# Factored self-attention as guest work of a cross attention: shifted keys and values moved by DMA, with separate tiles and chains

## The chip, the cores and the metric

The kernel runs on one core of a Trainium2 chip, as one launch. The metric is the device time of that launch in microseconds (us), the median of several executions. TensorE (PE) multiplies matrices, VectorE (DVE), ScalarE (ACT) and GpSimd (POOL) work on tiles in on-chip memory (SBUF) and on matmul results (PSUM), and SyncE (SP) issues most DMA transfers. The engines run in parallel. Each executes its own instructions in order and waits on semaphores for the others.

## The reference

A pre-norm decoder of twelve layers works on x, 8 batches x 256 rows x 128 channels in fp32, with a context of 8 x 512 x 128. Each layer is `x = x + layer(layernorm(x))`; attention has 16 heads of 8 channels. Three layers matter here.

```
x = x + L1_ffn(_layernorm(x))        # r = sigmoid(xr @ Wr.T); out = r * (relu(xk @ Wk.T)**2 @ Wv.T)
                                     # xr, xk: mixes of a row with the row before it
x = x + L2_attn(_layernorm(x))       # q, k, v = x @ W_qkv + b_qkv, 16 heads
                                     # softmax(where(fenwick_mask, q k^T * scale, -inf)) v, then W_proj
x = x + L2_xattn(_layernorm(x), ctx) # softmax(q k^T * scale) v over 512 context rows, no mask
```

In the mask of `L2_attn` row i sees itself and the rows i - 1, i - 2, i - 4, ..., i - 128. So a query has at most nine keys, at offsets 0, 1, 2, 4, 8, 16, 32, 64 and 128, and the layer can be computed from nine shifted copies of keys and values with no matrix of scores. That is what "factored" means in this document. Keys at negative rows are masked by a large negative number.

## The kernel before, in words

x lies in SBUF as 16 tiles of 128 rows (two to a batch), and its layernorm, transposed, as `E.xt(b)`, 128 channels x 256 rows. `E.xt(b, o)` is the same shifted by o rows.

**The head loop.** The second cross attention, `_l2_xattn` (L773), runs `_heads_attention` (L469): a loop over 128 head steps t, 16 for each of 8 batches. At step t it computes the scores of head t twice. First with queries on partitions, two matmuls `mh_sps` of 128x512, from which DVE takes the row maxima (`mh_nm`, L533). Every fourth step POOL splits four heads' maxima (`mh_hi`, L540), TensorE transposes them (`mh_mps`), and a DMA on ACT's queue writes them as two more rows of the queries. Eight steps behind, the scores come again with keys on partitions (`mh_bsps`), less the maxima, and ACT takes their exponential (`mh_e`, L587). Every fourth step `mh_ops` sums values over keys. In the steps h = 6 to 13 of batch b the keys, queries and values of batch b + 1 are projected and spread over partitions by twelve DMAs of SP (L425, L430). All matmuls and transposes go through `hd.mm` and `hd.turn_over` (L451, L454), which keep TensorE in the order in which the program is written; on the other engines a scheduler orders the instructions by their dependences.

**The guest.** The loop carries other layers' work between its own instructions: a generator, `guest`, is advanced `pace(t)` times a step (`visit`, L706), here 1.25. This guest is `rest()` in `_middle` (L1242): `_l1_ffn` for batch pairs 1 to 3, `_l2_attn` for batches 2 to 7, then the rounding of weights of a later layer (`_l2_ffn_weights`). Batches 0 and 1 of `_l2_attn` were done before the loop. Batch b + 1 must be finished by the guest before step h = 9 of batch b; if it is not, the loop visits until it is (L695).

**The factored attention before**, `_l2_attn` (L1082), handles one tile of 128 rows at a time. It projects queries (`fa_q`), then, for each pair of offsets, keys and values of the shifted rows by matmuls of 128x256 into PSUM (`fa_kvps`, L1113): 8 for the upper and 9 for the lower tile of a batch. DVE multiplies keys by queries out of PSUM (`fa_pr`, L1114), ACT copies the values (`fa_v`, L1117). DVE sums over the channels of a head (L1123) and does the softmax over offsets (L1124 to L1134), POOL weights the values (L1136) and adds offsets 4 to 7 on 0 to 3 (L1138), and DVE adds the rest (L1144 to L1148). A transpose, the output matrix `wo`, the residual (L1156) and the next layernorm follow.

Of the kernel before, what the change touches and what calls it, by code (L numbers as in the profile page):

```python
# [30 lines left out]
F32 = mybir.dt.float32  # L31
# [23 lines left out]
OFFS = (0, 1, 2, 4, 8, 16, 32, 64, 128)  # L55
# [166 lines left out]
def _run(steps):  # L222
    for _ in steps:
        pass
# [120 lines left out]
class _Heads:  # L345
# [30 lines left out]
    def third(self, ctx):  # L376

        pool = ctx.enter_context(self.E.tc.tile_pool(name="hd3", bufs=1, side="right"))
        q = pool.tile([P, H, S], F32R, name="mh_q2")
        for i in range(0, H, 4):  # L380
            self.E.nc.scalar.copy(
                q[:, i : i + 4, :].rearrange("p h n -> p (h n)"), self.E.plain[:, 0:1].to_broadcast([P, 4 * S])
            )
        self.q.insert(0, q)

    def begin(self, layer, keys, bias=True):

# [395 lines left out]
def _l3_masks(E, ctx):  # L783

    nc = E.nc
    pool = ctx.enter_context(E.tc.tile_pool(name="km", bufs=1))
    mk = ctx.enter_context(E.tc.tile_pool(name="kmb", bufs=2))
    kb = pool.tile([P, B, 2, P], BF16, name="km")
    kt = pool.tile([P, B, 2], F32, name="km_t")
    with E.tc.tile_pool(name="km_raw", bufs=1) as rp:  # L790
        raw = rp.tile([P, B * S], I32, name="km_raw")
        nc.sync.dma_start(raw, E.ins["key_mask"].to_broadcast([P, B * S]))
        flat = kb.rearrange("p b i k -> p (b i k)")
        for i in range(0, B * S, 512):
            nc.vector.tensor_scalar(flat[:, i : i + 512], raw[:, i : i + 512], 0.0, NEG, ALU.is_equal, ALU.mult)
        rt = rp.tile([P, B * 2], I32, name="km_rt")
        nc.sync.dma_start(rt, E.ins["key_mask_t"])
        nc.vector.tensor_scalar(kt.rearrange("p b i -> p (b i)"), rt, 0.0, NEG, ALU.is_equal, ALU.mult)

    cq = pool.tile([P, 3, P], F32, name="km_cq")  # L800
    ck = pool.tile([P, 3, P], F32, name="km_ck")
    for c, pattern, cm in ((cq, -1, 1), (ck, 1, -1)):
        nc.gpsimd.memset(c, 0.0)
        for i in (0, 2):
            nc.gpsimd.affine_select(
                out=c[:, i, :], in_=c[:, i, :], compare_op=ALU.is_ge, fill=NEG, base=0,
                pattern=[[pattern, P]], channel_multiplier=cm,
            )
# [227 lines left out]
def _l1_ffn(E, ctx, side="left"):  # L1036
    nc, W = E.nc, E.w("L1_ffn")
    wk = ctx.enter_context(E.tc.tile_pool(name="rk", bufs=1, side=side))
    rest = wk.tile([P, 2], F32, name="rk_rest")
    for i, n in enumerate(("mu_r", "mu_k")):  # L1040
        nc.vector.tensor_scalar(rest[:, i : i + 1], W(n), -1.0, 1.0, ALU.mult, ALU.add)

    def unit(g):
        mixed = []
        for i, n in enumerate(("mu_r", "mu_k")):
            t = wk.tile([P, 2, S], F32, name="rk_t")
            nc.vector.tensor_scalar(t, E.xt2(g, 1), rest[:, i : i + 1], None, ALU.mult)
            m = wk.tile([P, 2, S], F32, name=f"rk_m{i}")
# [127 lines left out]
    return through  # L1176


def plain_pe(E):

    E.mm, E.transpose = E.nc.tensor.matmul, E.nc.tensor.transpose
    E.turn_over = lambda out, in_: E.nc.tensor.transpose(out, in_, E.ident)


def _middle(E, names, then):

    nc = E.nc
    plain_pe(E)  # L1190
    banks = lambda to, name, bufs, side="left": to.enter_context(
        E.tc.tile_pool(name=name, bufs=bufs, space=PSUM, side=side)
    )
    if names != MIDDLE:
        for n in names:
            with ExitStack() as scope:
                pg = E.mid_ln = banks(scope, "mid_pg", 6)
                E.banks = SimpleNamespace(fa=pg, rk=pg, ln=pg)
                unit = {
                    "L0_ffn": _l0_ffn, "L1_attn": _l1_attn, "L1_xattn": _l1_xattn, "L1_ffn": _l1_ffn,  # L1200
                    "L2_attn": _l2_attn,
                }[n](E, scope, *([pg] if n in MIDDLE[:3] else []))
                if n == "L2_attn":
                    _run(unit(0, 4))
                    continue
# [553 lines left out]
```

## Time and profile before

| | |
|---|---|
| median of 3 runs | 1801.41 us (1801.25 to 1802.14) |
| profiled execution | 1797.04 us |
| its span | 1795.3 us, mean granted TensorE clock 0.913 |
| second cross attention, first to last maxima | 910.8 to 1280.6 us |
| start of each batch's first step | 910.8, 960.7, 1008.6, 1061.2, 1108.6, 1162.5, 1218.6, 1253.5 us |
| SP queue | 44,720 packets, 56.99 MB, 12.0% of 16 DMA engines' span |

The profile is that of one execution, and its span is the time from the first to the last instruction; the execution's own time is 1.7 us longer. A "busy" time is the sum of an engine's instruction durations. A group such as `fa_kvps<-w_L_attn,xt 128x256 x204` names the written tile, what is read, the shape and the count; after the bar stand busy us and mean ns of one, and behind the next bar the idle time of the engine just before these instructions and what ended it. One fp32 matmul shows as two records, so x204 are 102 matmuls. A wait "A <- B: 28.5, 12, 3.8" is that A stood 28.5 us in all, 12 times, at most 3.8 us, and that B ended it. In the stage's stretches the columns are: stretch, its length, busy us (instructions) of PE, PEld (weight loads), DVE, ACT and POOL, granted clock of TensorE, share of the DMA engines, GB/s.

### The profile page before, as it was taken

The page shows a single profiled execution, that of the slowest core. Times are in us where ns is not written, and L with a number is a line of the kernel's source. Part 1 is how long each engine was busy: PE and PEld are TensorE (multiplying, and loading weights), DVE is VectorE, ACT ScalarE, POOL GpSimd, SP SyncE. Part 2 cuts the span into 40 slices and gives each one's busy share as a digit, 9 for nine tenths or more (in the row PEclk, how much of TensorE's full clock was granted, in tenths as well). Part 3 has the DMA queues.
Part 4 walks back from the last instruction along what each step waited for, and adds up shares of the span by engine and source line. Part 5 has one row for each costly group of instructions (what it writes and reads, how often), then busy time and mean ns, then how long its engine had stood idle before and what let it go on. Part 6 is the DMA issues. An engine that isn't in the chain of part 4 may idle for free. (4 is left out here: it accounts for less than half of the span.)

```text
span 1795.3 us, 29269 instructions
## 1 busy us (share of the span) xinstructions
PE 1476.0 (82%) x10103; PEld 1067.2 (59%) x10141; DVE 1149.9 (64%) x3861; ACT 871.3 (49%) x1806; POOL 502.6 (28%) x998
## 2 busy tenths in 40 slices
PE   5689999999989989787468888878846889898986
PEld 3456677766655556455346666656515677677753
DVE  4567666765636676777467776767566656466656
ACT  7245445555642345222635655456644556455531
POOL 3122222121111121323323333332113443344321
PEclk9899999999999999886779999989957999899997
DMA  4011101114100000000111001111002321122100
GB/s 152 13 36 35 25 15 37 35 28 150 23 1 1 1 1 1 0 1 1 24 46 32 24 22 37 37 37 45 10 3 66 101 53 37 52 58 54 29 1 24
DMA packets 47235, 60.42 MB, mean 34 GB/s; under 512 B 5232, under 2 KB 36976, under 8 KB 46448
## 3 DMA queue, kind: packets, MB, share of 16 engines
q1 hardware_dynamic: 44720, 56.99, 12.0%
q8 instruction: 80, 1.31, 0.3%
q10 hardware_dynamic: 2368, 1.57, 0.3%
q14 instruction: 67, 0.55, 0.1%
HBM read 14.50 MB, written 1.05 MB: 9 GB/s over the span
## 5 line engine op out<-in xcount | busy, mean ns | idle before, releaser
L451 PE MATMUL mh_sps<-mh_k,mh_q 96*128 96x512 f32 (+2 forms) x1024 | 323.7, 398 | 54.2 <-DMA mh_q<-mh_qp 24.1
L451 PE MATMUL mh_bsps<-mh_q,mh_k 128*128 128x256 f32 (+1 forms) x1536 | 355.1, 337 | 7.1 <-ACT mh_e L587 4.1
L587 ACT ACTIVATE mh_e<-mh_bsps 128x512 f32<-128x512 f32 x512 | 281.0, 599 | 118.0 <-PE mh_bsps L451 110.7
L451 PEld LDWEIGHTS mh_bsps<-mh_q,mh_k 128*128 128x128 f32 x1536 | 267.9, 199 | 32.2 <-issue 6.9
L451 PEld LDWEIGHTS mh_sps<-mh_k,mh_q 96*128 96x128 f32 x1024 | 173.1, 203 | 102.1 <-issue 44.6
L514 DVE CUSTOM_DVE_ANT_0 mh_rest<-mh_sps,mask_b 128x512 bf16<-128x512 f32 x256 | 167.2, 684 | 84.2 <-PE mh_sps L451 81.0
L451 PE MATMUL mh_ops<-mh_e,mh_v 128*32 128x256 f32 (+1 forms) x3072 | 193.7, 373 | 1.3 <-DVE mh_nm L514 0.8
L533 DVE TENSOR_REDUCE mh_nm<-mh_sps 128x1 f32<-128x512 f32 x256 | 165.1, 681 | 33.7 <-PE mh_sps L451 33.2
L574 ACT ACTIVATE mh_e<-mh_bsps 128x384 f32<-128x384 f32 x256 | 118.7, 493 | 59.5 <-PE mh_bsps L451 36.2
L197 POOL TENSOR_SCALAR ln_rstd<-ln_mv 128x2 f32<-128x2 f32 x96 | 22.0, 229 | 401.2 <-DVE ln_mv L195 400.9
L451 PEld LDWEIGHTS mh_ops<-mh_e,mh_v 128*32 128x32 f32 x3072 | 94.2, 111 | 66.1 <-ACT mh_e L574 5.5
L540 POOL CAST mh_hi<-mh_nm 128x8 fp32r<-128x8 f32 x128 | 24.8, 194 | 340.8 <-DVE mh_nm L514 208.9
L514 DVE CUSTOM_DVE_ANT_0 mh_rest<-mh_sps,causal 128x128 bf16<-128x128 f32 (+1 forms) x256 | 79.4, 352 | 53.9 <-PE mh_sps L451 51.3
L514 DVE CUSTOM_DVE_ANT_0 mh_rest<-mh_sps,km_q 128x128 bf16<-128x128 f32 (+1 forms) x256 | 79.5, 350 | 46.4 <-PE mh_sps L451 44.6
L215 ACT COPY xt<-ln_ps 128x256 f32<-128x256 f32 x96 | 36.0, 375 | 127.3 <-PE ln_ps L454 67.8
L552 ACT CAST mh_m<-mh_mps 8x256 fp32r<-8x256 f32 x128 | 46.1, 360 | 101.7 <-PE mh_mps L454 100.3
L620 ACT COPY mh_osb<-mh_ops 128x256 f32<-128x256 f32 x128 | 47.6, 372 | 83.3 <-PE mh_ops L451 83.1
L885 ACT ACTIVATE moe_si<-moe_gps 128x512 f32<-128x512 f32 x64 | 38.0, 597 | 102.0 <-PE moe_gps L883 81.3
L451 PE MATMUL mh_bsps<-mask_t,ident 128*128 128x512 bf16 x219 | 85.0, 388 | 0.4 <-ACT mh_e L587 0.4
L883 PE MATMUL moe_ups<-xt,w_L_ffn 128*128 128x512 f32 x128 | 68.9, 621 | 7.0 <-ACT moe_si L885 4.8
L454 PE MATMUL mh_mps<-ident,mh_nx 128*8 128x128 f32 x256 | 50.9, 281 | 28.8 <-POOL mh_nx L543 24.2
L201 DVE TENSOR_SCALAR ln_z<-x,ln_mv,ln_rstd 128x128 f32<-128x128 f32 x128 | 41.9, 368 | 50.5 <-POOL ln_rstd L198 50.5
(360 smaller groups left out, 3109.6 us busy)
## 6 DMA issues: line engine op xcount, KB each, us to landing
mh_k<-mh_kp SPq DMA_DIRECT2D x64, 256.0 KB
mh_q<-mh_qp SPq DMA_DIRECT2D x256, 64.0 KB
mh_k<-mh_kp SPq DMA_DIRECT2D x64, 128.0 KB
w_L_ffn<-in_w_L_ffn SPq DMA_DIRECT2D x2, 1558.0 KB
w_L_attn<-in_w_L_attn SPq DMA_DIRECT2D x2, 1056.0 KB
ctx_t<-in_ctx_t SPq DMA_DIRECT2D x4, 512.0 KB
mh_q<-mh_m ACTq DMA_DIRECT2D x128, 8.0 KB
w_L_ffn<-in_w_L_ffn SPq DMA_DIRECT2D x2, 687.0 KB
```

What stands on the lines that cost most here:

```text
L201: (engine or nc.vector).tensor_scalar(z[:, q, :], E.x[:, 2 * b + q, :], mv[:, q, 0:1], rstd[:, q : q + 1], ALU.subtract, ALU.mult)
L215: E.nc.scalar.copy(E.xt(b), ps.rearrange("p q t -> p (q t)"))
L451: return self.E.tc.keep_in_program_order(self.E.nc.tensor.matmul(*a, **kw))
L454: return self.E.tc.keep_in_program_order(self.E.nc.tensor.transpose(*a))
L514: nc.vector.tensor_tensor_reduce(rest[:, : scores.shape[1]], scores, lowered, -1.0, -FLOOR, ALU.add, ALU.min, accum_out=at)
L533: nc.vector.tensor_reduce(u.nm[:, c, col], ps, AX.X, ALU.max, negate=True)
L552: nc.scalar.copy(m, ps[:8].rearrange("p c q -> p (c q)"))
L574: nc.scalar.activation(e, ps, AF.Exp, scale=scale)
L587: nc.scalar.activation(e, ps, AF.Exp, scale=scale)
L620: nc.scalar.copy(osbs[b][:, u4 % 2, :], ops)
L883: nc.tensor.matmul(ps, W("w13")[:, o : o + P], xt, start=True, stop=True)
L885: nc.scalar.activation(si, pgate, AF.Silu)
```

## The change

1. In the guest, batches 2 to 7 of the factored attention are done by a new function, `_l2_attn_moved`, a batch (both tiles) at a time. It projects keys and values of each row once, and makes the eight shifted copies by SBUF-to-SBUF DMAs of SP, 15 for the keys and 15 for the values of a batch. Keys `fm_k` and values `fm_v` have one tile each, 128 x (2 x 9 x 128) fp32, whose rows before the start of a batch are zeroed once. The bias is added before the copies.
2. Keys and values are two chains of steps; each visit advances both by one. The chain of keys (`weigh`) carries `_l1_ffn` ahead of it and ends with the softmax weights of a batch. The chain of values (`apply`) waits for those in program order, weights both halves on POOL, and finishes the batch.
3. The pace of the guest in `_l2_xattn` goes from 1.25 to 1.6.
4. `_l1_ffn` puts `rk_k` and `rk_r` into the buffers of its mixed inputs. The pool of the first `_l2_attn` is closed before the guest's own pools are opened.
5. The causal additive blocks of layers `L3_attn` and `L3_xattn` are no longer built by `_l3_masks` within `L3_attn` (two memsets and four selects of POOL): the transposed one, `E.causal_t`, is built with the first heads' setup in `L2_ffn` (a memset and two selects), and `E.causal[0]` stands in for the other.

```diff
 def _l2_xattn(E, ctx):
-    _heads_attention(E, ctx, guest=guest, known=(0, 1), pace=lambda t: 1.25)
+    _heads_attention(E, ctx, guest=guest, known=(0, 1), pace=lambda t: 1.6)
...
-    cq = pool.tile([P, 3, P], F32, name="km_cq")
-    ck = pool.tile([P, 3, P], F32, name="km_ck")
-    for c, pattern, cm in ((cq, -1, 1), (ck, 1, -1)):
...
+    cq, ck = E.causal[0], E.causal_t
...
-        k = wk.tile([P, 512], F32, name="rk_k")
+        k = wk.tile([P, 512], F32, tag="rk_m1", name="rk_k")
...
-        r = wk.tile([P, 4, D], F32, name="rk_r")
+        r = wk.tile([P, 4, D], F32, tag="rk_m0", name="rk_r")
...
+    for a in (k, v):
+        nc.scalar.copy(a[:, 0, 1:, :].rearrange("p o c -> p (o c)"), E.plain[:, 0:1].to_broadcast([P, (NO - 1) * D]))
...
+    def move(a):
+        moves = []
+        for i, o in enumerate(OFFS):
+            if 0 < o < P:
+                moves.append((a[o:, :, i, :], a[: P - o, :, 0, :]))
+                moves.append((a[:o, 1, i, :], a[P - o :, 0, 0, :]))
+            elif o:
+                moves.append((a[:, 1, i, :], a[:, 0, 0, :]))
+        for i in range(0, len(moves), 3):
+            for to, of in moves[i : i + 3]:
+                nc.sync.dma_start(to, of)
+            yield
+        for _ in range(4):
+            yield
+
+    def weigh(b):
+        E.pre_add(b, W("bo"))
+        q = wk.tile([P, 2, D], F32, name="fm_q")
+        for s in range(2):
+            ps = E.banks.fa.tile([P, 2 * D], F32, tag="g", name="fm_qkps")
+            E.mm(ps, E.xt(b)[:, s * P : s * P + P], W("wqkv")[:, : 2 * D], start=True, stop=True)
+            nc.vector.tensor_tensor(k[:, s, 0, :], ps[:, D:], W("b")[:, D : 2 * D], ALU.add)
+            nc.vector.tensor_tensor(q[:, s, :], ps[:, :D], W("b")[:, :D], ALU.add)
+        at.projected = b
+        yield
+        yield from move(k)
+        while b > at.used + 2:
+            yield
+        sc = wk.tile([P, 2, NO, H], F32, name="fm_sc")
+        for s in range(2):
+            nc.vector.tensor_tensor(k[:, s, :, :], k[:, s, :, :], q[:, s : s + 1, :].to_broadcast([P, NO, D]), ALU.mult)
+            yield
+            nc.vector.tensor_reduce(sc[:, s, :, :], heads(k[:, s, :, :]), AX.X, ALU.add)
+            yield
...
+    def apply(b):
+        while b > at.projected:
+            yield
...
+        nc.vector.tensor_tensor(v[:, :, 0, :], ps, row, ALU.add)
+        yield
+        yield from move(v)
+        while b not in weights:
+            yield
+        sc = weights.pop(b)
+        for s in range(2):
+            nc.gpsimd.tensor_tensor(
+                heads(v[:, s, :, :]), heads(v[:, s, :, :]), sc[:, s, :, :].unsqueeze(3).to_broadcast([P, NO, H, DH]),
+                ALU.mult,
+            )
+
+            nc.gpsimd.tensor_tensor(v[:, s, :4, :], v[:, s, :4, :], v[:, s, 4:8, :], ALU.add)
+        at.used = b
+        for _ in range(5):
+            yield
+        o = wk.tile([P, 2, D], F32, tag="fm_q", name="fm_o")
+        nc.vector.tensor_tensor(v[:, :, :2, :], v[:, :, :2, :], v[:, :, 2:4, :], ALU.add)
+        nc.vector.tensor_tensor(o, v[:, :, 0, :], v[:, :, 1, :], ALU.add)
+        nc.vector.tensor_tensor(o, o, v[:, :, 8, :], ALU.add)
+        yield
...
+        chain = keys()
+        for done in values():
+            yield done
+            next(chain, None)
...
+        if guest:
+            last.close()
...
-            yield from fa(1, 3, _l1_ffn(E, own))
+            rk = _l1_ffn(E, own)
+            if guest:
+                yield from _l2_attn_moved(E, own)(2, B, rk)
+            else:
+                yield from fa(1, 3, rk)
```

More of the change, by code (lines that the diff above doesn't have):

```diff
@@ L384, in third @@
         self.q.insert(0, q)
+        t = self.E.causal_t = pool.tile([P, 3, P], F32, name="causal_t")
+        self.E.nc.gpsimd.memset(t, 0.0)
+        for i in (0, 2):
+            self.E.nc.gpsimd.affine_select(
+                out=t[:, i, :], in_=t[:, i, :], compare_op=ALU.is_ge, fill=NEG, base=0,
+                pattern=[[1, P]], channel_multiplier=-1,
+            )
     def begin(self, layer, keys, bias=True):
@@ L798, in _l3_masks @@
         nc.vector.tensor_scalar(kt.rearrange("p b i -> p (b i)"), rt, 0.0, NEG, ALU.is_equal, ALU.mult)
-    cq = pool.tile([P, 3, P], F32, name="km_cq")
-    ck = pool.tile([P, 3, P], F32, name="km_ck")
-    for c, pattern, cm in ((cq, -1, 1), (ck, 1, -1)):
[L803 to L808, printed above, removed]
+    cq, ck = E.causal[0], E.causal_t
     def key_bias(b):
@@ L1047, in unit @@
             nc.vector.tensor_scalar(t, E.xt2(g, 1), rest[:, i : i + 1], None, ALU.mult)
-            m = wk.tile([P, 2, S], F32, name=f"rk_m{i}")
+            m = wk.tile([P, 2, S], F32, tag=f"rk_m{i}", name=f"rk_m{i}")
             nc.vector.scalar_tensor_tensor(m, E.xt2(g), W(n), t, ALU.mult, ALU.add)
@@ L1176, in _l2_attn, with _l2_attn_moved, through, keys @@
     return through
+def _l2_attn_moved(E, ctx):
+    nc, W = E.nc, E.w("L2_attn")
+    one = ctx.enter_context(E.tc.tile_pool(name="fm1", bufs=1))
+    wk = ctx.enter_context(E.tc.tile_pool(name="fm", bufs=2))
+    scale = DH ** -0.5
+    NO = len(OFFS)
+    shape = [P, 2, NO, D]
+    k, v = one.tile(shape, F32, name="fm_k"), one.tile(shape, F32, name="fm_v")
+    for a in (k, v):
+        nc.scalar.copy(a[:, 0, 1:, :].rearrange("p o c -> p (o c)"), E.plain[:, 0:1].to_broadcast([P, (NO - 1) * D]))
+    heads = lambda a: a.rearrange("p o (h d) -> p o h d", d=DH)
+    weights, at = {}, SimpleNamespace(projected=-1, used=-1)
+    def move(a):
[31 more added lines that the diff above has]
+            yield
+        nc.vector.tensor_tensor(
+            sc[:, 0, :, :], sc[:, 0, :, :], W("fenwick").unsqueeze(2).to_broadcast([P, NO, H]), ALU.add
+        )
+        red = wk.tile([P, 2, H], F32, name="fm_red")
+        wide = red.unsqueeze(2).to_broadcast([P, 2, NO, H])
+        by_head = sc.rearrange("p s o h -> p s h o")
+        nc.vector.tensor_reduce(red, by_head, AX.X, ALU.max)
+        nc.vector.tensor_tensor(sc, sc, wide, ALU.subtract)
+        nc.scalar.activation(sc, sc, AF.Exp, scale=scale)
+        yield
+        nc.vector.tensor_reduce(red, by_head, AX.X, ALU.add)
+        nc.vector.reciprocal(red, red)
+        nc.vector.tensor_tensor(sc, sc, wide, ALU.mult)
+        weights[b] = sc
+        yield
+    def apply(b):
+        while b > at.projected:
+            yield
+        ps = E.banks.fa.tile([P, 2, D], F32, tag="g", name="fm_vps")
+        for s in range(2):
+            E.mm(ps[:, s, :], E.xt(b)[:, s * P : s * P + P], W("wqkv")[:, 2 * D :], start=True, stop=True)
+        row = W("b")[:, 2 * D :].unsqueeze(1).to_broadcast([P, 2, D])
+        nc.vector.tensor_tensor(v[:, :, 0, :], ps, row, ALU.add)
[4 more added lines that the diff above has]
+        sc = weights.pop(b)
+        for s in range(2):
+            nc.gpsimd.tensor_tensor(
+                heads(v[:, s, :, :]), heads(v[:, s, :, :]), sc[:, s, :, :].unsqueeze(3).to_broadcast([P, NO, H, DH]),
+                ALU.mult,
+            )
+            nc.gpsimd.tensor_tensor(v[:, s, :4, :], v[:, s, :4, :], v[:, s, 4:8, :], ALU.add)
+        at.used = b
+        for _ in range(5):
+            yield
+        o = wk.tile([P, 2, D], F32, tag="fm_q", name="fm_o")
+        nc.vector.tensor_tensor(v[:, :, :2, :], v[:, :, :2, :], v[:, :, 2:4, :], ALU.add)
+        nc.vector.tensor_tensor(o, v[:, :, 0, :], v[:, :, 1, :], ALU.add)
+        nc.vector.tensor_tensor(o, o, v[:, :, 8, :], ALU.add)
+        yield
+        ps = E.banks.fa.tile([P, 2, P], F32, tag="g", name="fm_tps")
+        for s in range(2):
+            E.turn_over(ps[:, s, :], o[:, s, :])
+        ot = one.tile([P, 2, P], F32, name="fm_ot")
+        nc.scalar.copy(ot, ps)
+        yield
+        ps = E.banks.fa.tile([P, 2, D], F32, tag="g", name="fm_yps")
+        for s in range(2):
+            E.mm(ps[:, s, :], ot[:, s, :], W("wo"), start=True, stop=True)
+        E.add(b, ps)
+        z = _norm(E, b)
+        yield
+        yield
+        yield
+        _normed(E, b, z, E.banks.ln, E.turn_over)
+        yield b
+    def through(first, end, ahead):
+        at.projected = at.used = first - 1
+        def keys():
+            for b in range(first, end):
+                if b % 2 == 0:
+                    yield from ahead(b // 2)
+                yield from weigh(b)
+        def values():
+            for b in range(first, end):
+                yield from apply(b)
+        chain = keys()
+        for done in values():
+            yield done
+            next(chain, None)
+    return through
```

## The prediction

> **What bounds the kernel now.** I read the page's busy shares first, then the stage that the change touches (the second cross attention, whose 128 head steps run from 910.8 to 1280.6 us by the starts of their maxima, DVE L533), cut into its batches, then that stage's groups by shape, and last its waits.
>
> ```profile
> span 1795.3 us, 29269 instructions
> ...
> PE 1476.0 (82%) x10103; PEld 1067.2 (59%) x10141; DVE 1149.9 (64%) x3861; ACT 871.3 (49%) x1806; POOL 502.6 (28%) x998
> ```
>
> TensorE leads over the kernel, but not fully. The chain that ended last reaches only into the final feed-forward layer and says nothing of this stage. So I go to the stretches: us, then busy time of PE, PEld, DVE, ACT, POOL (instructions), granted clock, DMA share, GB/s.
>
> ```profile
> 910.00:961.00 51.00, 38.58 (x221) 27.13 (x221) 38.06 (x92) 20.71 (x43) 16.83 (x29) 0.89 0.13 32
> ...
> 1219.00:1254.00 35.00, 31.59 (x239) 22.62 (x239) 25.97 (x62) 23.51 (x51) 8.12 (x22) 0.95 0.24 57
> 1254.00:1281.00 27.00, 26.68 (x241) 18.95 (x240) 20.27 (x42) 18.92 (x40) 2.83 (x12) 1.00 0.01 2
> 910.00:1219.00 309.00, 255.49 (x1794) 186.20 (x1794) 229.56 (x593) 165.79 (x362) 109.98 (x188) 0.93 0.14 32
> ```
>
> Sixteen head steps alone take 27 us with TensorE 99% busy (1254 to 1281). The six batches that carry the guest work take 309 us, 51.5 each, with PE at 83%, DVE at 74%. TensorE is the bound there, with DVE close behind; 53 us are PE's idle time. Where they come from:
>
> ```profile
> DVE fa_v L1144 <- POOL fa_v L1138: 28.5, 12, 3.8
> PEld mh_sps L451 <- DVE mh_nm L533: 28.2, 39, 5.1
> ...
> PE mh_sps L451 <- DVE mh_nm L533: 14.5, 9, 4.6
> ...
> PE mh_sps L451 <- DMA mh_q<-mh_qp: 7.6, 1, 7.6
> ```
>
> (total us, times, longest.) DVE stands in its queue on POOL's weighted values (12 tiles, 28.5 us); behind it stand the maxima of the heads, and TensorE waits for those. The guest's attention is on all three engines:
>
> ```profile
> L451 PE MATMUL fa_kvps<-w_L_attn,xt 128*128 128x256 f32 x204 | 55.6, 398 | 6.7 <-DVE x L1156 4.7 <-ACT fa_v L1117 1.6 <-DVE fa_q L1102 0.3
> ...
> L1114 DVE TENSOR_TENSOR fa_pr<-fa_kvps,fa_q 128x256 f32<-128x256 f32 x48 | 19.8, 416 | 3.0 <-PE fa_kvps L451 2.8
> L1117 ACT COPY fa_v<-fa_kvps 128x256 f32<-128x256 f32 x48 | 17.4, 369 | 25.2 <-DVE fa_pr L1114 25.2
> L1138 POOL TENSOR_TENSOR fa_v<-fa_v 128x512 f32<-128x512 f32 x12 | 15.3, 1274 | 0.6
> ...
> L1136 POOL TENSOR_TENSOR fa_v<-fa_v,fa_sc 128x1152 f32<-128x1152 f32 x6 | 13.1, 2190 | 20.6 <-DVE fa_sc L1134 12.3 <-DVE ln_mv L195 8.4
> ...
> L1123 DVE TENSOR_REDUCE fa_sc<-fa_pr 128x144 f32<-128x1152 f32 x6 | 8.1, 1348 | 0.1
> ```
>
> **The change, part by part.** Six batches (2 to 7) are converted.
>
> TensorE. The 102 shifted key-value products go (204 records; a pair of records fills about 0.515 us in the timeline, so 102 x 0.515 = 52.5 us), and 12 query products of 128x128 with them (4.6 us, x24 records). New are 12 of 128x256 (12 x 0.515 = 6.2) and 12 of 128x128 (12 x 0.28 = 3.4). Net -47.5 us of PE work in the bounding stretch: 255.5 becomes 208.
>
> DVE. Gone are two halves' products, reduces and softmax on one tile each: 19.8 + 1.7 products, 15.4 reduces (L1123), about 50 us of small softmax, bias and fold instructions; 86.8 us in all from the rows. New per batch: four bias adds (4 x 0.28), two products and two reduces of 128x1152 (4 x 1.35, by the L1123 row; the product has no row at this width), the softmax once on 128x288 (2.5), folds, bias and residual (2.4): 11.4, so 68.5 for six. Net -18 us: 229.6 becomes 211. The product's ends: 1.2 to 2.4 us (twice, if reading two SBUF operands beside POOL halves its rate), so 0 to +12 us over 12; I take 1.35.
>
> ACT loses 19 us of value copies (L1117) and gains two fills of about 1.04 us each; it is off the path. POOL: 45.4 us of multiply and fold become 12 x (2.19 + 1.27) = 41.5, but in blocks of two halves, 6.9 us, instead of 3.5. The heads' minima (L540, 0.2 us each) queue behind that block. They feed exponentials that run eight steps later, some 18 us, which covers it; uncovered, 6.9 less the 3.3 that it costs now, 3.6 us a batch.
>
> SP. 180 SBUF-to-SBUF copies are new, 30 a batch. One issue on SP takes 0.61 us in this trace, so 15 take 9.2 us per tensor. They share SP's queue with twelve key and query spreads per batch (0.61 to 1.28 us each), on which the heads of the next batch depend. SP has little else here. Spreads and copies overlap at batches 5 to 7 (steps 41 to 45, 74 to 77 of the new order); a spread then lands up to 9 us later, against three to seven steps (6 to 16 us) of slack. I count nothing for it; uncovered it is the 7.6-us wait on mh_q of the fence, perhaps three times: 0 to 23 us.
>
> How long a moved tensor takes. By the rows: 918 KB in 512-byte packets, about 1,800, at the 27 ns that this trace's 512-byte packets take, over 16 engines is 3 us, so SP's issuing decides: 10 us. A rule speaks against it: the Trainium skill, "DMA: Bandwidth & Descriptors", section "Why a DMA increments its semaphore by 16 and not by 1", says that a transfer from SP or ACT uses the largest number of engines up to 16 that divides the slowest dimension; 127 partitions go on a single engine, and a smaller number uses the lowest-numbered ones. The offset-1 copy is 127 rows x 2 = 254 packets on engine 0: 6.9 us; with its shares of the others (62 for the 124-row copy, 84 for the rest) engine 0 carries 400 packets, 10.8 us. The trace agrees with the rule in one place: the first queue of ACT, 2,368 packets, adds up only if the two-row copies of the minima go over two engines. Copies reuse eight semaphores in turn, so the ninth waits for the first: about 15 us from the first issue to the last landing. The chain leaves eight visits at 1.6 per step, five steps of 2.4 us: 12. So the product waits nothing by the row, 3 us by the rule. As DVE executes in order, the maxima behind it wait, then mh_sps on PE. I take the rule, with 2 us of PE time for each of six key copies: 12 us (range 0 to 36 with values' sums late as well, which wait only behind POOL).
>
> A new DVE block. In the built program's DVE order, batch 2's whole chain (products, reduces, softmax, 10.5 us) and its sum, which waits for POOL's 6.9 us, stand together after step 15's maxima and ahead of step 16's. Before, the same place waited 3.7 us. PE has three score banks of lead, so of the some 17 us I count 8 us. At batches 5 and 6 nine such instructions (8.5 us) stand together: 4 us each in the sum below for what exceeds a bank's lead, 8 in all.
>
> Pace 1.25 to 1.6 lets the guest end at step 93 instead of 104 and cancels three forced visits in steps 41 and 73. Work is compressed, not removed: nothing. The causal blocks: a memset and two selects move to the feed-forward layer and two memsets (0.42) and four selects (0.29 to 0.47) leave POOL in the third attention; POOL is 28% busy, no one waits: zero, at most 2 us either way. Shared mixing tiles make the ACT relu wait for its product's reader, same engine order as now: zero, at most 1 us a pair, 3.
>
> Sum on the profiled execution: -47.5 + 12 + 8 + 8 = -19.5 us. DVE's 18 us do not add to PE's. But the waits of the old arrangement (28.5 us in 12 on POOL, half of which reached PE) become six instead of twelve: -7. So -26 to -27; 1797.04 - 27 = 1770. The median of the runs, 1801.41, is 4.4 above the profiled execution; the same step from it gives 1774.
>
> **Rivals.**
> A. All cover holds: PE work is the bound, at its 83%: 208 / 0.83 = 251 instead of 309, so -58; some of it is lost to DVE at 84%: -45 to -58, 1743 to 1756. For it: PE is at 99% when alone. Against: DVE then has as much work as PE in each batch (35 us of each).
> B. DVE becomes the bound. 211 us of DVE work in blocks of 8 to 17 us; at the 74% it reaches now that is 285 us, -24; at 70%, 301, -8; 1777 to 1796. For it: the block at step 16. Against: most of DVE's idle time today is waiting for PE and POOL.
> C. Slower: engine 0 becomes the bound. 800 packets of two tensors per batch and about 8 us of spreads lie on it. At 27 ns that is 30 us; 46 ns, this trace's 1-KB packets, gives 45, still under 51.5; from 54 ns on it exceeds the batch of before, and the products, and all maxima behind them, run at its pace. This trace's 2-KB packets between tiles take 162 ns at the median, which speaks for such prices; at 60 ns it is 56 us a batch, 6 x 4.8 = +29: 1830. Against: 512 bytes are a quarter of those, and packets of that size show 27.
> D. The change does not reach the bound: if the new waits cancel the PE work, within 4 us of 1801. It follows from my sum with late copies at 36 us and both blocks fully on PE (+34): -47.5 - 7 + 36 + 34 = +15, so no change lies within reach.
>
> **How the numbers follow.** My sum 0.40, A 0.14, B 0.16, D 0.08 (no change), C with its neighbours 0.22. Faster by over 0.2% (3.6 us, about what a measurement of this kernel can tell from no change): 0.40 + 0.14 + most of B, 0.67; within: 0.08; slower: 0.25 (C, and 0.03 of the far ends of B and D). The range reaches from inside A, 1745, to inside C, 1818.
>
> **What would show it.** The fa_kvps group of batches 2 to 7 gone and PE about 47 us lower in the stage; stage length 340 to 345 us instead of 370. Waits "DVE on a DMA of the moved keys" of 2 to 4 us six times are my 12 us; none at all speaks for A; waits over 10 us in every batch speak for C. Step 16 as the longest gap between maxima is the block. I am wrong if PE's granted clock, 0.93 in this stretch, falls with more idle (each 0.01 is near 3 us), if POOL's 6.9-us blocks reach the exponentials, or if the two-SBUF products take well over 1.35 us.

## The result and the profile after

The changed kernel takes 1851.06 us (median of 4 runs, 1847.54 to 1852.10) where the kernel before, on the same chip, took 1801.78 us (1801.25 to 1805.66): a ratio of 1.0253, interval 1.0234 to 1.0272. It is slower by 49 us. The forecast of 1774 us had the wrong sign, and the time lies outside its range. First the page, in the lines that answer to those of before:

```profile
span 1849.9 us, 28944 instructions
...
PE 1464.2 (79%) x9923; PEld 1051.2 (57%) x9961; DVE 1150.5 (62%) x3753; ACT 857.5 (46%) x1742; POOL 502.3 (27%) x983
```

No engine has more work than before (DVE 0.6 us more, the others less) and the span is 54.6 us longer, so the time is in waiting. The starts of the maxima, step by step, put it all in the second cross attention: first to last maxima took 370 us and now take 426 (907.2 to 1332.8). Its stretches, with the columns of before:

```profile
907.00:978.00 71.00, 35.53 (x186) 23.72 (x184) 37.17 (x74) 18.42 (x34) 16.09 (x26) 0.72 0.21 54
...
1304.00:1333.00 29.00, 28.67 (x245) 19.74 (x244) 20.49 (x42) 18.91 (x39) 2.57 (x12) 0.94 0.01 3
907.00:1273.00 366.00, 244.70 (x1601) 170.45 (x1603) 230.59 (x501) 150.67 (x301) 111.77 (x177) 0.79 0.23 57
```

In the six batches with guest work PE has 193 records fewer than before (1601 against 1794), yet its busy time falls by 11 us only. The granted clock is 0.79 in place of 0.93, and each matmul left takes longer (an `mh_ops` of 128x256: 452 ns in place of 394). The lower clock goes with the idle time, 121 us in place of 53. DVE has not gained 18 us either (230.6 against 229.6; more of the later layer's weight rounding, some 5 us, lies in this stretch than before). The last stretch, with no guest, is nearly as it was (29 us in place of 27). What fills the idle time, from the waits of 900 to 1350 us:

```profile
PE mh_sps L459 <- DMA mh_q<-mh_qp: 33.4, 5, 11.7
...
POOL fm_v L1259 <- DMA fm_v<-fm_v: 28.1, 3, 13.4
...
ACT mh_e L595 <- DMA fm_v<-fm_v: 25.0, 3, 14.1
...
PE mh_sps L459 <- DVE mh_nm L541: 16.9, 12, 4.5
...
DVE fm_v L1269 <- POOL fm_v L1264: 16.3, 5, 6.9
...
PE mh_bsps L459 <- ACT mh_e L595: 15.7, 4, 13.7
...
DVE fm_k L1225 <- DMA fm_k<-fm_k: 15.2, 4, 5.8
```

The queries of the next batch come later than before (33 us in place of 7.6), DVE and POOL wait for moved keys and values, and ScalarE's exponentials wait for a copy with which they share no data. Of the 33.4 us, 7.5 stand at the start of the stage, as before; the other 25.9 stand ahead of the steps 48, 64, 80 and 112. The line of the exponentials is the strangest. The timeline of one case shows how it comes about; first SP's queue (start, length, what, how many in the group), then ScalarE's:

```profile
925.09 7.37 SPq L1205 DMA_DIRECT2D fm_k<-fm_k  x4
932.58 7.81 SPq L1205 DMA_DIRECT2D fm_v<-fm_v  x3
940.44 1.41 SPq L1205 DMA_DIRECT2D fm_k<-fm_k  x2
```

```profile
932.40 0.36 ACT L560 CAST mh_m<-mh_mps 8x256 fp32r<-8x256 f32 x1
932.67 0.58 ACT L595 ACTIVATE mh_e<-mh_bsps 128x512 f32<-128x512 f32 x1
946.73 0.62 ACTq L562 DMA_DIRECT2D mh_q<-mh_m  x1
947.39 2.57 ACT L595 ACTIVATE mh_e<-mh_bsps 128x512 f32<-128x512 f32 x5 [14.14 <-DMA fm_v<-fm_v]
```

The minima `mh_m` are ready at 932.8, but the DMA that writes them goes out at 946.7. In the trace's records every DMA of SP and of ScalarE in this stage uses one of the same eight completion semaphores in turn, and it waits until that semaphore's previous DMA has landed. The previous one was here the value copy for offset 4 (124 rows), issued at 942.57 and landed at 946.65. ScalarE's small DMA stood behind it, and five exponentials stood behind that DMA. TensorE had no free buffer for more scores and stood 13.7 us (the last but one line of the waits). SP was stuck as well: its seven issues from 925.1 to 940.4 take 15.2 us, of which issuing alone is 7 x 0.61 = 4.3. In the trace's packets, 38 or so of 512 bytes go per us from 934 to 940, one after the other at 27 ns: two offset-1 copies of 254 packets, keys then values, both on a single engine (the semaphore of each gets one update when it lands, that of a 112-row copy 16).

This stall of SP is not a wait for a semaphore. In all twelve cases the issue that follows an offset-1 copy takes 4.6 to 6.1 us, although its own semaphore's previous DMA had landed before it started. They are the long ones of these two groups (count, then ns of the shortest, the median and the longest), first in the changed kernel, then in the one whose offset-1 copies go in two parts (the first experiment below):

```profile
L1205 SPq DMA_DIRECT2D fm_k<-fm_k x90: 503/672/5397, 925.1 to 1187.4; - x90
L1205 SPq DMA_DIRECT2D fm_v<-fm_v x90: 584/674/6118, 932.6 to 1224.6; - x90
```

```profile
L1209 SPq DMA_DIRECT2D fm_k<-fm_k x102: 521/663/1290, 928.4 to 1180.7; - x102
L1209 SPq DMA_DIRECT2D fm_v<-fm_v x102: 513/660/1262, 931.6 to 1218.1; - x102
```

The twelve take 58.9 us together, and everything that SP issues later, spreads and other copies, moves back with them.

The new compute groups are as costed (900 to 1350 us):

```profile
L1259 POOL TENSOR_TENSOR fm_v<-fm_v,fm_sc 128x1152 f32<-128x1152 f32 x12 | 26.9, 2257 | 38.1 <-DMA fm_v<-fm_v 28.1 <-DVE fm_sc L1241 10.0
L1225 DVE TENSOR_TENSOR fm_k<-fm_k,fm_q 128x1152 f32<-128x1152 f32 x12 | 15.9, 1352 | 15.2 <-DMA fm_k<-fm_k 15.2
L1227 DVE TENSOR_REDUCE fm_sc<-fm_k 128x144 f32<-128x1152 f32 x12 | 15.8, 1341 | 0.0
```

### The profile page after: what moved, and what is told of

The parts are those of the page before. It is cut to its first block, busy times and chain, and to the rows that moved or that the text cites. A ratio compares the mean times of both kernels' runs of the same rounds, so it can differ in the third digit from the quotient of the medians.

```text
span 1849.9 us, 28944 instructions
## 1 busy us (share of the span) xinstructions
PE 1464.2 (79%) x9923; PEld 1051.2 (57%) x9961; DVE 1150.5 (62%) x3753; ACT 857.5 (46%) x1742; POOL 502.3 (27%) x983
## 5 line engine op out<-in xcount | busy, mean ns | idle before, releaser
L459 PE MATMUL mh_sps<-mh_k,mh_q 96*128 96x512 f32 (+2 forms) x1024 | 329.9, 405 | 89.5 <-DMA mh_q<-mh_qp 50.9
L595 ACT ACTIVATE mh_e<-mh_bsps 128x512 f32<-128x512 f32 x512 | 276.9, 599 | 153.5 <-PE mh_bsps L459 103.8
L459 PEld LDWEIGHTS mh_bsps<-mh_q,mh_k 128*128 128x128 f32 x1536 | 275.0, 205 | 46.1 <-ACT mh_e L595 19.2
L459 PE MATMUL mh_ops<-mh_e,mh_v 128*32 128x256 f32 (+1 forms) x3072 | 204.1, 389 | 0.9 <-DVE mh_nm L522 0.8
L462 PE MATMUL ln_ps<-ident,ln_z 128*128 128x128 f32 x128 | 33.9, 339 | 53.0 <-DVE ln_z L201 38.1
L894 PEld LDWEIGHTS moe_dps<-w_L_ffn,moe_act 128*128 128x128 f32 x512 | 66.2, 205 | 15.9 <-issue 7.7
```

What stands on the lines that cost most here:

```text
L459: return self.E.tc.keep_in_program_order(self.E.nc.tensor.matmul(*a, **kw))
L462: return self.E.tc.keep_in_program_order(self.E.nc.tensor.transpose(*a))
L595: nc.scalar.activation(e, ps, AF.Exp, scale=scale)
L894: nc.tensor.matmul(ps[:, t, :], act[:, c, t * P : t * P + P], W("w2")[:, o : o + P], start=c == 0, stop=c == 1)
```

## The experiments

Each kernel was timed in three rounds beside the kernel before on the same chip; times are medians. "Queries late" below is the wait of `mh_sps` on the DMA of `mh_q`; 7.5 us of it, at the very start of the stage, are there in every kernel. A caution for what follows: the new function issues three DMAs a visit, so a kernel with another number of copies a tensor also has another number of visits between a tensor's projection and its use (five for the 15 copies of the changed kernel, six for 17, four for 10, three for 9, each with four empty visits behind). Where two kernels differ so, it is said.

**First four: where the 49 us are.** The theories on record are ONE ENGINE, SP QUEUE and COMPUTE ORDER.

```diff
-                moves.append((a[o:, :, i, :], a[: P - o, :, 0, :]))
+                if o in (1, 4):
+                    moves.append((a[o : o + 112, :, i, :], a[:112, :, 0, :]))
+                    moves.append((a[o + 112 :, :, i, :], a[112 : P - o, :, 0, :]))
+                else:
+                    moves.append((a[o:, :, i, :], a[: P - o, :, 0, :]))
```

> The changed kernel, but the copy for offset 1 (127 rows) goes as 112 + 15 rows and the one for offset 4 (124 rows) as 112 + 12, so that no large copy lies on one or four DMA engines; bytes are the same, issues are 17 a tensor in place of 15. Theory ONE ENGINE (the 254 packets that go one after the other for 6.9 us hold up whatever reuses a completion semaphore, ScalarE's own DMA of the minima and SP's spreads): most of the 49 us comes back, 1800 us or less, and the three waits of mh_e on fm_v's DMA (25 us) and half of the 33 us on mh_q go. Theory SP QUEUE (too many issues in one in-order queue, those that wait for DVE at its head): two more issues a tensor, 1845 to 1860. Theory COMPUTE ORDER (DVE and POOL blocks, pace): unchanged, 1845 to 1855.

Measured: 1827.68 us, ratio 1.0151 (1.0129 to 1.0173). This lies between the theories: 23.4 us of the loss come back, and 26 do not, in a kernel with one visit a tensor more. The wait of the exponentials falls from 25.0 to 2.2 us, as ONE ENGINE said, but the late queries stay (907 to 1250 us):

```profile
PE mh_sps L459 <- DMA mh_q<-mh_qp: 31.1, 3, 13.0
```

Second, the pace:

```diff
-    _heads_attention(E, ctx, guest=guest, known=(0, 1), pace=lambda t: 1.6)
+    _heads_attention(E, ctx, guest=guest, known=(0, 1), pace=lambda t: 1.25)
```

> The changed kernel with the guest's pace back at 1.25. ONE ENGINE and SP QUEUE: copies have a quarter more time until they are read, and the spreads meet them elsewhere, so 5 to 20 us less, 1831 to 1846. COMPUTE ORDER with the pace as its main part: most of the loss is gone, below 1815. If the guest's deadlines (forced visits) matter: slower than 1851.

Measured: 1862.82 us, 1.0334 (1.0317 to 1.0351), 12 us slower than the changed kernel. The new pace as the main cause has fallen, and so has the guess that more time for the copies would help: the late queries grow to 74.3 us (900 to 1350 us). The outcome named for missed deadlines came; gaps between maxima of 15.9 and 11.8 us stand ahead of the steps 25 and 41, where the loop forces visits, but no run parts their cost from that of the copies.

Third, no copies:

```diff
             for to, of in moves[i : i + 3]:
-                nc.sync.dma_start(to, of)
+                pass
```

> The changed kernel without its 180 copies: the shifted keys and values stay zero or stale, so the factored attention of six batches isn't computed (two more fills of SBUF by ScalarE are in it). ONE ENGINE and SP QUEUE: what is left is 47 us less PE work and the DVE block at step 16, 1755 to 1785. COMPUTE ORDER: the loss stays, 1835 or more.

Measured: 1789.24 us, 0.9925 (0.9909 to 0.9941). Taking away only the copies gains 61.8 us: the copies are the loss. But the kernel that is left is 13.0 us faster than before, 4 us above what the first two theories expected, where my sum without late copies has 38.5 (-47.5 + 16 - 7). Its waits say where that went (907 to 1250 us):

```profile
PE mh_sps L459 <- DVE mh_nm L541: 32.9, 16, 14.1
...
DVE fm_v L1270 <- POOL fm_v L1265: 26.2, 6, 7.0
```

In each of six batches DVE stands for POOL's block, up to 7.0 us, with the maxima behind it. As in the changed kernel, the longest gap is ahead of step 16: 18.5 us without copies (943.9 to 962.4), 20.3 with them (957.7 to 978.0).

Fourth, `_l2_attn_moved` taken out and the old function and pace put back:

> The changed kernel with the old factored attention and the old pace: only the shared mixing buffers and the causal blocks of the change remain. All three theories: 1798 to 1805. If the smaller edits carry the loss: above 1815.

Measured: 1804.77 us, 1.0027 (1.0011 to 1.0042). The small edits cost 2 to 8 us by the interval, not nothing, but not the loss.

**Next four: what of the copies still costs after the split.** The theories are SP QUEUE, LANES (shared semaphores) and LATE PRODUCT. All but the last kernel start from the split one.

```diff
-                moves.append((a[:o, 1, i, :], a[P - o :, 0, 0, :]))
```

> The split kernel (1827.7 us) without its seven small copies a tensor (the rows that come over from the tile above, so those shifted rows stay zero and the result isn't the reference's; two more fills are in it): 10 issues of SP a tensor in place of 17, and 6% less data. Theory SP QUEUE (what is left of the copies' cost is the number of issues in one in-order queue, copies and spreads behind each other): most of the 38 us between split and no copies goes in proportion, 1805 to 1814. Theory LANES (copies wait at SP's head for the semaphore that ScalarE's minima DMA had taken): fewer collisions, 1808 to 1820. Theory LATE PRODUCT (DVE stands at the head of its queue for copies that need their time anyway): 1820 or more.

Measured: 1804.31 us, 1.0002 (0.9995 to 1.0009). Dropping 84 issues and 7% of the bytes (127 of 1,793 rows) gives 23.4 us, 0.28 us each. So few bytes speak for the number of transfers: as issues on SP, and as turns on the eight semaphores. That is not shown, though, since this kernel also has two visits a tensor fewer than the split one, and the run after the next shows that visits alone can cost as much.

```diff
-        nc.scalar.dma_start(u.r.q[TOP : TOP + 2, h0 : h0 + 4, :].bitcast(F32), m.bitcast(F32))
+        (nc.gpsimd if E.heads.layer == "L2_xattn" else nc.scalar).dma_start(
+            u.r.q[TOP : TOP + 2, h0 : h0 + 4, :].bitcast(F32), m.bitcast(F32)
+        )
```

> The split kernel with the DMA of the minima on GpSimd's queue in this stage, which has semaphores of its own: SP's copies no longer reuse one that ScalarE's DMA holds. LANES: 10 us or more less, 1805 to 1817. SP QUEUE and LATE PRODUCT: 1822 to 1830; if GpSimd's issuing costs more than it frees (32 issues behind its 7-us blocks), 1835 or more.

Measured: 1813.39 us, 1.0047 (1.0030 to 1.0063), 14.3 us less than the split kernel, and the late queries fall from 31.1 to 7.5 us. LANES holds for this part, in both directions: ScalarE no longer waits for SP's DMAs, nor SP for ScalarE's (43.1 us of SP's waiting ahead of its query spreads are gone).

```diff
-        for _ in range(4):
+        for _ in range(8):
             yield
```

> The split kernel with eight empty visits behind a tensor's copies in place of four, so that products and weighted values are placed some 2.5 steps later. LATE PRODUCT: DVE's 25 us on the keys' DMA go, 1805 to 1815. SP QUEUE: the waits on mh_q stay and the chain of a batch is longer, so 1822 to 1835. If the guest then misses its deadlines, forced visits make it slower than 1835.

Measured: 1865.27 us, 1.0335 (1.0317 to 1.0353), 38 us slower than the split kernel. LATE PRODUCT is refuted: given more time, DVE still stands 19.7 us for moved keys in place of 25.0, and the late queries and the waits on moved values grow. The queries are late ahead of the steps 32, 48, 64, 80 and 96, by 11 to 14 us each, so the longer chain lies worse against the spreads; at step h = 9, where forced visits would stand, there is no such gap. The number of visits alone thus moves the time by 38 us (900 to 1330 us):

```profile
PE mh_sps L459 <- DMA mh_q<-mh_qp: 69.1, 6, 13.5
...
DVE fm_v L1273 <- POOL fm_v L1268: 57.7, 4, 17.8
...
POOL fm_v L1263 <- DMA fm_v<-fm_v: 50.2, 4, 13.6
```

The fourth is the kernel without copies and without POOL's two instructions per half (L1259, L1264 of the changed kernel).

> The kernel without copies (1789.2 us) and also without POOL's weighting and first fold of the values (the factored attention of six batches isn't computed). If POOL's 6.9-us blocks, on which DVE stood 26 us, are what kept that kernel from the predicted gain: 1765 to 1775. If DVE would have found no other work: 1782 or more.

Measured: 1751.89 us, 0.9706 (0.9692 to 0.9721), 37.4 us less than without copies. This is below all that was expected. POOL's blocks were worth more than the 26 us that DVE is seen to stand for them. The rest is about what PE's busy time falls by, 11.5 us for the same 1609 records, at a granted clock of 0.92 in place of 0.87; first the six batches without copies, then without POOL's instructions too:

```profile
906.00:1206.00 300.00, 229.35 (x1609) 162.84 (x1613) 227.98 (x502) 151.22 (x302) 109.02 (x177) 0.87 0.14 33
```

```profile
906.00:1174.00 268.00, 217.85 (x1609) 152.89 (x1612) 223.75 (x502) 150.69 (x302) 66.85 (x153) 0.92 0.16 37
```

**Next four: another way for the copies.** Each tensor goes once to device memory behind 128 rows of zeros; eight loads of 128 rows bring it back shifted.

```diff
+        d = through_dram["fm_dk" if a is k else "fm_dv"]
+        rows = lambda o: d[P - o : 3 * P - o, :].rearrange("(s p) c -> p s c", p=P)
+        moves = [(rows(0), a[:, :, 0, :])]
         for i, o in enumerate(OFFS):
-            if 0 < o < P:
-                moves.append((a[o:, :, i, :], a[: P - o, :, 0, :]))
-                moves.append((a[:o, 1, i, :], a[P - o :, 0, 0, :]))
-            elif o:
-                moves.append((a[:, 1, i, :], a[:, 0, 0, :]))
+            if o:
+                moves.append((a[:, :, i, :], rows(o)))
```

> The minima's DMA on GpSimd's queue in this stage (as in the kernel of 1813.4 us), and each tensor goes once to device memory, behind 128 rows of zeros, and comes back shifted in eight loads of 128 rows: 9 issues a tensor in place of 17, none on fewer than 16 engines; the loads wait for the store. SP QUEUE: 96 issues less at the 0.28 us that each of the 84 left-out ones was worth, 27 us: 1785 to 1795. If the way through device memory (store, then load, at the head of SP's queue) costs 2 us a tensor or more that reaches TensorE: 1800 to 1815.

Measured: 1789.76 us, 0.9924 (0.9895 to 0.9953): as fast as the kernel with no copies at all, and faster than the kernel before. The time lies in the SP QUEUE interval of 1785 to 1795, but with three visits a tensor fewer than the kernel of 1813.4 us and two fewer than the one without copies, the run does not show that the issues made the difference. The DMA waits of the first fence are gone or small (907 to 1250 us):

```profile
PE mh_sps L459 <- DVE mh_nm L541: 26.6, 13, 5.4
...
PE mh_sps L459 <- DMA mh_q<-mh_qp: 4.1, 1, 4.1
```

On that kernel, eight in place of five empty visits behind POOL's work:

> The same with eight empty visits in place of five between POOL's weighting and DVE's sum. If DVE's standing on POOL costs by its place in DVE's order alone: 8 to 20 us less than the former. If the chain of a batch is what decides (as four more visits behind the copies suggested, +38 us): 5 to 20 us more.

Measured: 1796.62 us, 0.9950 (0.9934 to 0.9967): 7 us slower, in the direction expected of the longer chain, though the two intervals meet. And, in place of that, the lower tile's weighting on DVE:

```diff
-        for s in range(2):
-            nc.gpsimd.tensor_tensor(
+        for s, engine in ((0, nc.gpsimd), (1, nc.vector)):
+            engine.tensor_tensor(
...
+            if s == 0:
+                yield
```

> The first of these with the upper tile's weighting and fold on POOL as before and the lower tile's on DVE, one visit later: POOL's block is 3.5 us, DVE has 12 us more work over six batches. POOL block as the cost (37 us when it was left out): 10 to 20 us less than the first. DVE as the bound: 0 to 12 us more.

Measured: 1788.20 us, 0.9909 (0.9892 to 0.9927), not told apart from the first. DVE's standing on POOL falls from 15.9 to 7.1 us, and about 12 us of work come to DVE.

> The kernel before with only the minima's DMA of this stage on GpSimd's queue. All theories: it has no copies to collide with, 1798 to 1806. If that queue is better by itself: 1790 or less, and the 14 us of the split kernel with it are no sign of shared semaphores.

Measured: 1804.78 us, 1.0000 (0.9990 to 1.0010). GpSimd's queue is no better by itself, so what it gave elsewhere is the collision. SP's query spreads wait for ScalarE's minima in the kernel before too (62.1 us in nine waits of SP), and without those waits nothing is gained. So in this kernel the shared semaphores cost nothing; in the split one, copies stood behind them.

**Next three: which queue, and which pace.** First the changed kernel with nothing but the minima moved:

> The changed kernel (1851 us, its 127-row copies on one engine) with nothing but the minima's DMA of this stage on GpSimd's queue. If the one-engine copies cost mainly because ScalarE stands at the head of its queue for a semaphore that such a copy holds (three waits, 25 us, at the exponentials): most of the split's 23 us and of the 14 us of the other queue come together, 1808 to 1825. If they cost mainly through SP's order and late products: 1835 to 1845.

Measured: 1830.53 us, 1.0163 (1.0132 to 1.0193), 20.5 us less. It lies between the two intervals; the exponentials' wait on copies is gone, and the late queries stay at 34.7 us. So the one-engine copies have two ways to TensorE: through ScalarE's queue (20.5 us by this kernel), and through SP's stalled queue, since splitting them still gives 17.1 us more (1830.53 to 1813.39, with one visit a tensor more): the twelve issues of 4.6 to 6.3 us are still in this kernel, and none over 1.6 us is in that of 1813.39.

> The kernel by way of device memory (1789.8 us) with the minima's DMA back on ScalarE's queue, so that it shares semaphores with SP's again. If sharing costs what it did in the split kernel: 1800 to 1806. If it costs only as long as copies land late: 1788 to 1796.

Measured: 1794.65 us, 0.9957 (0.9941 to 0.9973), 4.9 us more than with GpSimd's queue; the intervals meet. Sharing costs little here, where copies land soon.

> The kernel without copies (1789.2 us) at the old pace of 1.25 (the factored attention of six batches isn't computed). If the missing part of the predicted gain lies in compressing the guest into fewer steps: 1760 to 1780. If blocks of DVE and POOL cost the same at any pace: 1785 to 1793. If the guest now misses its deadlines: 1795 or more.

Measured: 1766.29 us, 0.9805 (0.9780 to 0.9831): 23 us less than at 1.6 and 37 below the kernel before. That is near the 38.5 us that my sum had without late copies, but the sum was for a pace of 1.6, so the agreement is in part luck.

**Last three: does that hold with copies?** The kernels by way of device memory at other paces.

> The kernel by way of device memory with the minima's DMA on GpSimd's queue (1789.8 us), at the old pace of 1.25. If without late copies the slower pace is worth what it was worth without copies (23 us): 1764 to 1775. If the longer chain of a batch, store and loads included, now misses the deadlines of the guest, as the changed kernel did at 1.25 (12 us slower than at 1.6): 1795 or more.

Measured: 1812.02 us, 1.0051 (1.0036 to 1.0066): no. It is 22 us slower than at 1.6, and 46 us slower than the kernel without copies at this pace. The queries are late by 10 us in all, 7.5 of them at the start as everywhere, so it isn't late spreads; what grew is DVE's standing for POOL's block, 7 us in each batch. Its waits first (900 to 1330 us), then those of the kernel without copies at the same pace (907 to 1250 us):

```profile
PE mh_sps L459 <- DVE mh_nm L541: 57.3, 14, 12.7
DVE fm_v L1274 <- POOL fm_v L1269: 44.0, 6, 7.5
```

```profile
DVE fm_v L1270 <- POOL fm_v L1265: 15.5, 6, 6.9
```

> The same with the lower tile's weighting on DVE. If POOL's 6.9-us blocks still hold DVE: 5 to 15 us less than the former. If DVE is the bound or nothing waits: within 3 us of it.

Measured: 1795.67 us, 0.9962 (0.9945 to 0.9979): with the lower half on DVE 16 of the 22 us come back. So POOL's block, placed as it is at this pace, is most of what costs.

> The kernel of the first run at a pace of 1.4. If the time depends smoothly on the pace: between 1.25 and 1.6, some 1773 to 1784. If placing against single steps decides: outside of these two.

Measured: 1787.61 us, 0.9921 (0.9894 to 0.9949). It is not between the two: at or below the kernel at 1.6, from which it isn't told apart, and well below the one at 1.25. Time does not follow the pace smoothly. With the first and the halved kernel of the way through device memory it forms a group of three between 1787.6 and 1789.8 us, 0.8 to 0.9% faster than before, that these rounds don't tell apart.

## Why the prediction was wrong

**The step that failed** is the account of the copies: "I take the rule, with 2 us of PE time for each of six key copies: 12 us", and before it, on the spreads in SP's queue, "I count nothing for it; uncovered ... 0 to 23 us". The copies cost 61.8 us, more than the upper ends of both ranges together (36 and 23). Of the some 76 us between forecast and result they are 50; the other 25 are the gain without copies, 13.0 in place of 38.5. I followed each copy only to the one instruction that reads it. The product was right: DVE stood 15.2 us for key copies, four times, where the rule gave 18. What I left out is who waits without reading: a DMA of ScalarE's that takes its turn on the same eight semaphores, and all exponentials behind it. I had written that copies reuse eight semaphores, but counted that among SP's own DMAs only. And I priced every issue of SP at 0.61 us, also the one behind a 127-row copy, which took 4.6 to 6.1. The collisions with the spreads of steps 41 to 45 and 74 to 77 that I named and counted at nothing came: the queries of the steps 48 and 80 were 8.2 and 11.7 us late. Two more, 4.2 and 1.8 us at the steps 64 and 112, I had not seen.

How 61.3 of the 61.8 us divide, by kernels, down to the one by way of device memory: ScalarE's turn 20.5 us (1851.06 to 1830.53), the one-engine copies beyond it 17.1 (to 1813.39), the number and form of transfers 23.6 (to 1789.76). In another order the shares differ: the split first gives 23.4, then the other queue 14.3. The two overlap, and each share has some 5 us of uncertainty (by the ratios instead of the medians the three are 16, 21 and 22 us). The last step changes number, source, shape and the visits of a batch's chain together; the kernel without the small copies alone gives 23.4 for 84 issues and two visits. So the first share is shown by a run that changes nothing else, the second nearly so, and the cause of the third stays open.

**The rule of the Trainium skill** ("DMA: Bandwidth & Descriptors", section "Why a DMA increments its semaphore by 16 and not by 1"), one engine for 127 rows, holds in this trace: one packet of 27 ns after the other, some 13 us for the two copies. My packet price was right, and the estimate of 6.9 us a copy too.

**Rival C** had the right sign for the wrong reason. It needed 54 ns a packet, so that engine 0's throughput limits a batch. Packets took 27 ns at the median, and 400 of them per tensor are 130 us for twelve tensors in a stretch of 366. So engine 0 was not full on average; what cost was time spent standing in two in-order queues, SP's behind each offset-1 copy and ScalarE's behind a semaphore. In rival B the upper end, 1796, should have been 1793 by its own 8 us.

**The PE work** went as listed by count: no `fa_kvps` in this stage, and 185 records fewer in the six batches without copies (1609 against 1794). Its size did not: PE's busy time falls by 26 us there, at a clock of 0.87, and by 38 without POOL's blocks, at 0.92, where I had 47.5 at the 0.93 of before.

**"Pace ... Work is compressed, not removed: nothing"** was wrong in size: without copies the new pace costs 23 us. With copies by device memory it gains 22. The placement of DVE's sum against POOL's block is behind the second (44.0 us of standing, and 16 us back with half the block); for the first the standing falls only from 26.2 to 15.5 us, so the rest is open.

**POOL's blocks.** I had the exponentials covered, and they are (no wait of ScalarE on POOL shows in the stage). But DVE's waits "become six instead of twelve: -7" took no account of the wait being twice as long; leaving the block out gave 37.4 us at the new pace. The block at step 16 was sized rightly for this order of instructions: a gap between maxima of 18 to 20 us, with and without copies, where it was 10.3 before (950.4 to 960.7), so 8 to 10 us against the 8 that I had counted. Most of it is POOL's block: without that the gap is 11.7 us. By way of device memory it is 10.7. **Causal blocks and mixing buffers**, predicted at zero and at most 5, cost 2 to 8. **The product** with two SBUF operands took 1352 ns (estimate 1350). **The clock**, 0.93 to 0.79, was named as a way to be wrong, and was.

Not settled: whether a small copy's 0.28 us come from its issue time, its turn on a semaphore, or the visits that go with it; what holds SP for 4 us and more behind an offset-1 copy; and why the kernel without copies gains 23 us at the old pace and that by way of device memory loses 22. A kernel with fewer copies and the old number of visits was not run. A larger set of semaphores was not tried.

## What to carry to other kernels

Before adding DMAs to a queue, list every DMA of any engine that takes turns with them on the same completion semaphores, and what stands behind each on its engine: a late copy can stop an engine that never reads it (14.1 us here). Look also at how long the issuing engine is held behind each transfer. Count transfers and their rows per engine, not bytes: at the pace of 1.6 the kernel with one store and eight whole-tile loads a tensor was as fast as one without copies, where fifteen copies, less data between tiles already on the chip, cost 62 us. At 1.25 it was 46 us behind, so such a price holds for one placing of the work. And when a multi-microsecond block moves to another engine, look in the built order for the instruction that waits for it and what is queued behind, since a different pace or one more visit can place it well or badly.

## What the runs showed of the hardware

The way through device memory was as fast as no copies at a pace of 1.6, 1789.76 against 1789.24 us, and not at 1.25, 1812.02 against 1766.29. Two DMA queues hold each other up through shared semaphores even where no data are shared: 14.1 us for a DMA of 8 KB. GpSimd's DMAs of the minima used eight other semaphores. The issue of SP behind a copy that runs on a single engine, 254 packets of 512 bytes, took 4.6 to 6.1 us in twelve of twelve cases, where the median issue took 0.67. TensorE's granted clock in the stage went with its idle time, though not along one curve: 0.93 with 53 us idle of 309, 0.92 with 50 of 268 without copies and without POOL's blocks, 0.87 with 71 of 300 without copies, and 0.79 with 121 of 366 in the changed kernel, but 0.86 with 105 of 327 in the kernel of 1813.39 us.
